# A decoder layer on one core: the summed weights of the first pair of queries are loaded ahead of the turned x1

## The chip, the core and the metric

The kernel runs on one core of a Trainium2 chip. A core has a matrix engine (TensorE, PE in the profile; its weight loads are shown as PEld), a vector engine (VectorE, DVE), a scalar engine (ScalarE, ACT), a general engine (GpSimd, POOL) and a queue engine (SyncE, SP) that here only issues transfers. Transfers are carried out by 16 DMA engines that all queues share. The metric is the time of one execution on the device in microseconds (us); the figure of a kernel is the median of its runs.

## The reference

One layer of a decoder, all in float32, with 8 sequences of 256 tokens and a width of 1024:

```python
x = _layernorm(x + attn(x, wq, wk, wv, wo))                     # causal, 32 heads of 32, 8 key heads, rotary
x = _layernorm(x + xattn(x, ctx, ctx, pos, mask, Wq, Wk, Wv, Wo))  # 32 heads of 128, 8 key heads, rotary, masked
x = _layernorm(x + ffn(x, ...))                                 # 256 memory slots: top 8, softmax, a gate
```

In the cross-attention the queries are `x @ Wq` with `Wq` of 1024 x 4096, and keys and values are `ctx @ Wk` and `ctx @ Wv` of 1024 x 1024. Then `out = softmax(q k / sqrt(128), masked) v` and `out @ Wo`, with `Wo` of 4096 x 1024.

## The kernel before

The work is staged in one pass over the self-attention (64 steps: 8 sequences of 8 steps) and one over the cross-attention (128 heads: 4 quarters of 512 tokens, 32 heads each). The first stage also computes, beside its own work, the keys and values of the cross-attention. The result of the first stage after its normalisation is called x1. It is turned tile by tile (`turn`: L397 transposes on TensorE, L398 copies on VectorE and ScalarE, L404 stores on ScalarE's queue) into x1T, since a projection wants the contracted dimension on the partitions.

Projections of the cross-attention save one multiplication in eight: two 128-wide outputs and two halves of the tokens are computed with seven block products instead of eight (`seven`, a scheme of Strassen's kind). The products are called p1, p2, p6, p5, p3, p7, p4, in this order. The token side needs the blocks B11, T3, B22, B21 of x1T (`load_blocks`, four loads of 512 KB, L642) and the sums T1, T2, T3, T4 of them (L646 to L649, on GpSimd for the first quarter). The weight side needs three kinds of tiles: the plain weights `a` of the pair's first output (p1 and p2), two tiles of summed weights `s24` and `s31` (p6 and p3; p5 and p7), which GpSimd has computed and stored in DRAM during the first stage, and half a tile of plain weights of the second output (p4). Each product is 4 matmuls of 128 x 128 by 128 x 256, which the profile counts as 8 (L757), into one bank of PSUM. What frees the bank is a copy on ScalarE for p1 (L776) and additions on VectorE for the others (L763). Two finished halves make a query of 512 tokens, which VectorE rotates with cos and sin (L730 to L734).

A pair of queries whose `seven` is called with `eager=True` loads `a` when its list of products is made, and not in p1. This is so for the first pair alone: `xa_early` makes it at the end of step 61, right before the loads of x1T, of cos and sin and of the first keys. The products themselves come later: p1, p2, p6, p5 at the end of step 62 and p3, p7, p4 with the first three of the next pair at the start of step 63.

The order of the work on TensorE, GpSimd and SyncE in the first stage is that of the program text (`manual_schedule`); VectorE's and ScalarE's is set by a scheduler, and GpSimd's last loads of the residual x1 (L119) belong to the second stage and are placed by it too. SyncE works through its queue strictly in order: a load that waits for a free buffer holds all loads behind it. Weights, turned tiles and a few others share one ring of 9 buffers of 512 KB (`w4`). The framework gives transfers issued by SyncE and ScalarE eight completion counters in turn, and a transfer waits until the previous holder of its counter has landed.

Around the change SyncE's queue has, in this order: plain weights of the first pair, x1T (4 loads), cos, sin, keys kT, `sa_wo` (4 loads of 512 KB for the last output projection of the self-attention, L364), the two summed tiles of the first pair, half a plain tile for p4, the plain weights of the second pair, its first summed weights, the mask (read by the mask bias, L695), its second summed weights. x1T is loaded into memory that the first stage's early pool gives back, so that its first load waits for the last work of that pool.

## Time and profile before

| | |
|---|---|
| runs | 3465.23, 3473.19, 3473.85 us; median 3473.19 |
| profiled execution | 3463.37 us, span 3461.6 us |
| TensorE busy | 3369.3 us, 97% of the span |
| VectorE, ScalarE, GpSimd busy | 61%, 35%, 30% |
| granted TensorE clock, mean | 0.988 |
| bytes moved | 626 MB, 181 GB/s over the span |

The profile is of one execution. An engine's busy time is a sum over the whole span, so it says which engine bounds the kernel and not what a single place costs. For that there are the chain of waits (the work that ended last, followed back from the end, each piece to what released it), the timeline of an engine or a queue, the waits summed by who waited for whom, and the busy times, granted clock and transfer rate of chosen stretches. The change touches the place where the first stage gives way to the second, 1100 to 1260 us after the start.

### The profile page before, as it was taken

The page shows a single profiled execution, that of the slowest core. Times are in us where ns is not written, and L with a number is a line of the kernel's source. Part 1 is how long each engine was busy: PE and PEld are TensorE (multiplying, and loading weights), DVE is VectorE, ACT ScalarE, POOL GpSimd, SP SyncE. Part 2 cuts the span into 40 slices and gives each one's busy share as a digit, 9 for nine tenths or more (in the row PEclk, how much of TensorE's full clock was granted, in tenths as well). Part 3 has the DMA queues.
Part 4 walks back from the last instruction along what each step waited for, and adds up shares of the span by engine and source line. Part 5 has one row for each costly group of instructions (what it writes and reads, how often), then busy time and mean ns, then how long its engine had stood idle before and what let it go on. Part 6 is the DMA issues. An engine that isn't in the chain of part 4 may idle for free.

```text
span 3461.6 us, 71080 instructions
## 1 busy us (share of the span) xinstructions
PE 3369.3 (97%) x27811; PEld 2443.5 (71%) x27811; DVE 2109.8 (61%) x6003; ACT 1202.3 (35%) x4030; POOL 1044.9 (30%) x1363
## 2 busy tenths in 40 slices
PE   8999999999999799999999999999999999999996
PEld 6787778787777567777767667667667766766763
DVE  4655556565565455665685666675666666566556
ACT  3444334333443343333233332233333323333224
POOL 3444655666665121111221111112111212121112
PEclk9999999999999899999999999999999999999998
DMA  7777788787886464444544344444444544344442
GB/s 254 236 258 250 269 268 279 257 273 258 296 271 221 156 215 141 143 135 134 171 149 140 123 134 142 150 137 156 138 128 133 167 142 147 128 132 135 129 146 98
DMA packets 269710, 626.36 MB, mean 181 GB/s; under 512 B 28992, under 2 KB 99792, under 8 KB 268480
## 3 DMA queue, kind: packets, MB, share of 16 engines
q1 hardware_dynamic: 194832, 441.00, 38.9%
q0 software_dynamic: 50032, 154.66, 13.8%
q10 hardware_dynamic: 24512, 26.15, 2.2%
q8 instruction: 221, 3.62, 0.4%
q14 instruction: 113, 0.93, 0.1%
HBM read 526.93 MB, written 94.77 MB: 180 GB/s over the span
## 4 chain that ended last, share of the span: by engine, by line
PE 87%; DVE 6%; DMA 2%; ACT 2%; POOL 2%; issue 2%; SPq 0%; POOLq 0%; DVEq 0%; ACTq 0%
PE mm L757 26%; PE mm L963 20%; PE mm L214 7%; PE mm L910 7%; PE mm L373 6%; PE sc L859 6%; PE mm L751 5%; PE sc L339 3%; PE mm L1241 2%; PE mm L243 1%; PE sc L273 1%; PE mm L1018 1%; POOL acc L992 1%; ACT att L295 1%; DMA w<-in_sa_wq 0%
## 5 line engine op out<-in xcount | busy, mean ns | idle before, releaser
L757 PE MATMUL mm<-x1T,w 128*128 128x256 f32 x3584 | 851.9, 382 | 13.7 <-DMA w<-xa_wq_sums 10.8
L757 PEld LDWEIGHTS mm<-x1T,w 128*128 128x128 f32 x3584 | 676.9, 190 | 199.0 <-issue 94.8
L963 PE MATMUL mm<-w,xoS 128*128 128x512 f32 x992 | 449.2, 595 | 0.0
L873 ACT ACTIVATE xatt<-xatt,nmax 128x256 f32<-128x256 f32 x512 | 257.2, 503 | 508.1 <-DVE nmax L868 496.2
L676 POOL DMA_DIRECT2D v<-v x256 | 150.9, 596 | 735.1 <-PE mm L910 617.1
L963 PE MATMUL mm<-w,xoT 128*128 128x512 f32 x744 | 338.1, 596 | 5.3 <-ACT xoT L918 4.1
L963 PEld LDWEIGHTS mm<-w,xoS 128*128 128x128 f32 x992 | 184.9, 190 | 193.1 <-issue 170.9
L214 PE MATMUL mm<-xT,w 128*128 128x256 f32 x1280 | 305.0, 395 | 3.1 <-DMA xT<-in_xT 2.9
L763 DVE TENSOR_TENSOR half<-mm,half 128x256 f32<-128x256 f32 x288 | 119.7, 416 | 291.1 <-PE mm L757 273.2
L214 PEld LDWEIGHTS mm<-xT,w 128*128 128x128 f32 x1280 | 245.4, 196 | 54.8 <-issue 19.0
L910 PEld LDWEIGHTS mm<-xat,v 32*128 32x128 f32 x8192 | 244.3, 187 | 53.4 <-issue 29.3
L929 POOL TENSOR_TENSOR xoS<-xoT 128x512 f32<-128x512 f32 x62 | 79.0, 1274 | 671.8 <-ACT xoT L918 671.5
L910 PE MATMUL mm<-xat,v 32*128 32x128 f32 x8192 | 270.2, 278 | 5.4 <-DVE acc L970 4.4
L295 ACT ACTIVATE att<-att,nmax 128x128 f32<-128x128 f32 (+1 forms) x512 | 225.5, 442 | 143.0 <-DVE nmax L290 142.8
L859 PE MATMUL sc<-kT,qT 128*128 128x256 f32 x1024 | 262.7, 380 | 0.0
L879 ACT ACTIVATE xatt<-xatt,rec 128x256 f32<-128x256 f32 x512 | 231.1, 499 | 88.0 <-DVE rec L877 87.6
L918 ACT COPY xoT<-mm 128x128 f32<-128x128 f32 x512 | 98.0, 276 | 470.2 <-PE mm L910 439.2
L763 DVE TENSOR_TENSOR raw<-mm,half 128x256 f32<-128x256 f32 x384 | 159.1, 414 | 159.3 <-PE mm L757 118.3
L423 POOL TENSOR_TENSOR ws<-ws 128x256 f32<-128x256 f32 x320 | 242.1, 757 | 26.2 <-DMA ws<-in_xa_wk 5.7
L963 PEld LDWEIGHTS mm<-w,xoT 128*128 128x128 f32 x744 | 138.7, 190 | 148.1 <-issue 127.3
L893 DVE STREAM_TRANSPOSE xat<-xatt 128x512 f32<-128x512 f32 x256 | 180.8, 707 | 74.6 <-ACT xatt L879 71.9
L373 PE MATMUL mm<-sa_wo,sa_oT 128*128 128x512 f32 x512 | 224.8, 592 | 0.0
(230 smaller groups left out, 4859.9 us busy)
## 6 DMA issues: line engine op xcount, KB each, us to landing
w<-xa_wq_sums SPq DMA_DIRECT2D x128, 512.0 KB, 3.6
w<-xa_wo_sums SPq DMA_DIRECT2D x124, 512.0 KB, 3.6
w<-in_xa_wo SPq DMA_DIRECT2D x97, 512.0 KB, 4.2
w<-in_sa_wq SPq DMA_DIRECT2D x64, 512.0 KB, 9.1
sa_wo<-in_sa_wo SPq DMA_DIRECT2D x64, 512.0 KB, 7.0
w<-in_xa_wq SPq DMA_DIRECT2D x64, 512.0 KB, 3.5
v<-v POOLq DMA_DIRECT2D x256, 128.0 KB, 3.1
w<-xa_wk_sums SPq DMA_DIRECT2D x32, 512.0 KB, 8.5
```

What stands on the lines that cost most here:

```text
L214: nc.tensor.matmul(ps[:, :S], lhsT=lhs[:, k, :], rhs=xT[:, k, :], start=(k == 0), stop=(k == KC - 1),)
L295: nc.scalar.activation(att[:, jj, lo:hi], att[:, jj, lo:hi], AF.Exp, bias=nmax[:, i : i + 1], scale=-1.0, accum_out=sums[:, i : i + 1],)
L373: nc.tensor.matmul(ps, lhsT=oTs[b * KC + c][:, tt * P : (tt + 1) * P], rhs=wos[b, half][c // 2][:, c % 2, :], start=(c == 0), stop=(c == K ...
L423: nc.gpsimd.tensor_tensor(out, in0, in1, op)
L757: nc.tensor.matmul(ps[:, :S], lhsT=w[:, k, :], rhs=rhs[:, k, :], start=(k == 0), stop=(k == 3))
L763: nc.vector.tensor_tensor(out, in0, in1, ALU.add)
L859: nc.tensor.matmul(sc[:, qt, :], lhsT=qT[:, q0 : q0 + P], rhs=kT[:, b * S : (b + 1) * S], start=True, stop=True,)
L873: nc.scalar.activation(att[:, qt, :], att[:, qt, :], AF.Exp, bias=nmax[:, qt : qt + 1], scale=-1.0, accum_out=sums[:, qt : qt + 1],)
L879: nc.scalar.activation(att[:, qt, :], att[:, qt, :], AF.Identity, bias=0.0, scale=rec[:, qt : qt + 1])
L893: self.nc.vector.transpose(self.ats[M, b][:, :, u].rearrange("p c t j -> p t c j"), self.atts[H][b].rearrange("p t (c j) -> p t c j", j=32),)
L910: nc.tensor.matmul(banks[i][:, :P], lhsT=v[rows, c, :], rhs=at[rows, c, :], start=(c == 0), stop=(c == BLOCKS - 1),)
L963: nc.tensor.matmul(ps, lhsT=oT[lhs][:, u, off + p * P : off + (p + 1) * P], rhs=w[:, u, :], start=(u == 0), stop=(u == 1),)
```

## The change

For the pair made with `eager=True` the two tiles of summed weights are now loaded where the plain ones are, when the list of products is made; p6 and p5 load them only for the other pairs. The loads themselves, their sizes and the products stay as they are. On SyncE's queue the two loads move from behind `sa_wo` to directly behind the plain weights, ahead of x1T.

```diff
         now = {}
         if eager:
             now["a"] = self.weights([P, KC, XA_D], self.a[name][2 * m])
+            for i, sums in enumerate(("s24", "s31")):
+                now[sums] = self.weights([P, KC, XA_D], self.wsums[name, m][i])
...
         def p6():
-            now["s24"] = self.weights([P, KC, XA_D], self.wsums[name, m][0])
+            if not eager:
+                now["s24"] = self.weights([P, KC, XA_D], self.wsums[name, m][0])
             ps = product(now["s24"][:, :4, :], "T2")
...
         def p5():
-            now["s31"] = self.weights([P, KC, XA_D], self.wsums[name, m][1])
+            if not eager:
+                now["s31"] = self.weights([P, KC, XA_D], self.wsums[name, m][1])
             ps = product(now["s31"][:, 4:, :], "T1")
```

In the changed program three more things stand elsewhere, as the scheduler and the turn of the counters set them: on GpSimd the load of x1's third residual tile (L119) comes ahead of the block sum T2 and not behind T4; on VectorE the mask bias comes behind the rotation of the second query and not ahead of that of the first; and the counters of the transfers from x1T to `sa_wo` are those of two places further on.

## The prediction

> **What bounds the kernel now.** I read the page first, then the chain of waits in order of time around the first pair of queries, then SyncE's queue, then stretches of the clock. The page says that TensorE is the bound, so a stall of TensorE is worth about its length:

> ```profile
> span 3461.6 us, 71080 instructions
> PE 3369.3 (97%) x27811; PEld 2443.5 (71%) x27811; DVE 2109.8 (61%) x6003; ACT 1202.3 (35%) x4030; POOL 1044.9 (30%) x1363
> PE 87%; DVE 6%; DMA 2%; ACT 2%; POOL 2%; issue 2%; SPq 0%; POOLq 0%; DVEq 0%; ACTq 0%
> ```

> The chain in order of time, from 1150 to 1203 us (columns: start, length, what). Two transfers follow one another with no TensorE work between them: a turned tile of x1 is stored, then summed weights are loaded, and only then does L757 go on.

> ```profile
> 1157.43 11.93 DMA x1T<-w
> ...
> 1171.34 9.08 DMA w<-xa_wq_sums
> 1180.42 0.14 issue
> 1180.56 14.00 PE mm L757 x56
> ```

> SyncE's queue in order of time (start, length of issuing, line, transfer): it is silent from 1104.85 to 1156.04; it stops again from 1160.15 to 1169.38; the summed weights are issued behind four loads of `sa_wo`.

> ```profile
> 1104.52 0.33 SPq L109 DMA_DIRECT2D w<-in_xa_wq  x1
> 1156.04 2.03 SPq L642 DMA_DIRECT2D x1T<-x1T  x4
> 1158.11 0.91 SPq L664 DMA_DIRECT2D cos<-tables  x1
> 1159.06 0.45 SPq L664 DMA_DIRECT2D sin<-tables  x1
> 1159.55 0.60 SPq L668 DMA_DIRECT2D kT<-kT  x1
> 1169.38 1.92 SPq L364 DMA_DIRECT2D sa_wo<-in_sa_wo  x4
> 1171.34 1.20 SPq L109 DMA_DIRECT2D w<-xa_wq_sums  x2
> 1172.58 1.21 SPq L109 DMA_DIRECT2D w<-in_xa_wq  x2
> ```

> SyncE's own waits name the second stop (total, times, longest): the store of the turned tile.

> ```profile
> SPq L364 <- DMA x1T<-w: 9.2, 1, 9.2
> ```

> The stretches (TensorE busy, granted clock, DMA share, GB/s): the idle time from 1169.8 to 1180.56 halves the clock, and it stays halved until 1184; the transfers meanwhile run full at 408 GB/s.

> ```profile
> 1142.00:1146.00 4.00, 1.03 (x7) 1.00 0.93 327
> 1146.00:1153.00 7.00, 5.36 (x100) 0.53 0.10 40
> 1173.00:1180.50 7.50, 0.00 (x0) 0.55 1.05 408
> 1180.50:1184.00 3.50, 3.44 (x8) 0.51 1.05 399
> 1184.00:1194.50 10.50, 10.50 (x52) 1.00 0.43 161
> ```

> Work that stands ready meanwhile, out of the timeline: it sets how early the next products could run.

> ```profile
> 1170.41 2.35 POOL L649 TENSOR_TENSOR x1T<-x1T 128x1024 f32<-128x1024 f32 x1
> 1171.15 0.56 ACT L398 COPY w<-mm 128x512 f32<-128x512 f32 x1
> 1173.01 0.35 ACT L776 COPY half<-mm 128x256 f32<-128x256 f32 x1
> ```

> **The change, part by part.** No instruction is added. Two 512 KB loads move.

> *The two loads.* They go directly behind the plain weights, ahead of x1T, cos, sin, kT and `sa_wo`. Their buffers were last read by a value product of step 58 and by the query projection L214, whose matmuls run from 1118.05 to 1121.77, so both are issued by about 1122, inside SyncE's silence. The eight such loads issued here before took 7.8 us (median) to land; by 1132 they are there. DMA share was 0.54 in 1118 to 1122 and 0.00 in 1122 to 1130, and TensorE waited for no transfer from 1100 to 1156. I take 0. If that cover were gone, 1.05 MB at 0.4 MB/us costs 2.6 us; a gain below 0 is excluded, since nothing there waits for them.

> *Queue places.* Transfers of SyncE and ScalarE take eight completion counters in turn, and each waits for the last holder of its counter. That is the 9.2 us wait: the first `sa_wo` shared one with the store issued at 1157.43. Two places further on, it is the sin load that stands behind that store, so sin, kT and all behind them go out when it lands: at 1169.36, or up to 1 us earlier, as 0.5 MB no longer competes with it. Sin is first read after p3, at about 1175.8, and lands by about 1172.5 (3 us of cover); kT is read at 1215.

> *POOL.* In the changed order the load of x1's third residual tile (0.55 us of issuing) stands ahead of the block sum T2. It waits for transposes that end at 1165.56, so T2 starts at 1166.2 instead of 1165.76 and ends at 1168.55, before p6 wants it at 1169.8: 0, with 1.2 us of cover. Its 512 KB now moves with the `sa_wo` loads from their start.

> *VectorE.* The mask bias (0.69 us) moves behind the second rope; VectorE is not on the path, and the bias is first read at 1216.83: 0.

> *TensorE, where the gain is.* A product takes 1.73 us at full clock. Before, seven (p6, p5, p3, p7, p4 and the next pair's p1, p2) ran from 1180.56 to 1194.48: 13.92 us against 7 x 1.73 = 12.1, so the halved clock cost 1.8. After:
> - p6 starts at 1169.8. p5 needs a bank freed by ScalarE at 1171.71, so 1171.8. p3 needs the L776 copy (1173.36), so 1173.5. p7 follows at 1175.3 and ends at 1177.0. Nothing here waits longer than 0.3 us.
> - p4 is late next: its plain weights (256 KB) were not moved. Ahead of them on the queue, after the restart, stand sin, kT and four `sa_wo`: 0.26 + 0.26 + 2.10 MB, and 0.26 of their own, 2.88 MB. Before, the first summed weights ended after 2.10 + 0.52 = 2.62 MB and landed at 1180.42. So p4's weights land 0.26 MB (0.65 us) later against a restart 0 to 1 us earlier: 1180.1 to 1181.1. Bounds from both sides: 1178.5, if the residual load is out of the way early, and 1183.5, if it and the second store keep half the engines. I take 1180.2, since the byte count is nearest to the row measured.
> - p4 and two more products are 5.2 us, plus the clock. TensorE idles 3.2 us (1177.0 to 1180.2). The row of 1142 to 1153 shows what such a gap does: idle from 1142.87 to 1145.85, and then 0.53. So again 1.8: end at 1187.2 instead of 1194.48.

> [...]

> Later work hangs on TensorE itself: `sa_wo` is reloaded when L373 has read it (1210.34), the values when the last transposes are done (1231.52), so it moves along. Sum: -7.3 us (-0.21%).

> **Against which time.** The profiled execution took 3463.37 us, 1.8 more than its span. The runs shown are 3465.23, 3473.19 and 3473.85, median 3473.19: with the profiled one, two levels some 9 us apart. -7.3 gives 3456.1 at the profiled level and 3465.9 from the median. A median of three new runs can fall at either, so I start from the mean of the four, 3468.9: 3462.

> **The rivals.** 0.3% (10.4 us) is about what a measurement of this kernel can tell from no change.
> - *Clock kept.* A gap of 3.2 us stays at full clock: -7.3 - 1.8 = -9.1, 3454 to 3464. [...] Against: the row above. [...]
> - *The whole stall goes.* p4's weights land by 1177.0: end 1182.2, -12.3, about 3457 to 3461. Against: 2.88 MB after 1169 at 0.4 MB/us needs 7.2 us and some 2 us to start and land.
> - *Given back.* The residual load and the second store take half the engines, p4 starts at 1183.5: -4, about 3465 to 3469. For it: before, this load began late, after `sa_wo`. Against: it is only 0.5 MB.
> - *Slower.* The second summed load waits for its buffer and holds x1T and all behind it in SyncE's queue, which is in order. Each us that the buffer comes free after 1156.04 then costs 1 us, less the 7.3: slower from 1163.3 on. If the buffer were the first turned tile's (read until 1169.36) it is 13.3 - 7.3 = +6; if the second one's (issued at 1171.74, 14.6 us to land), +23, some 3492. Against: the changed order gives it a buffer read last at 1121.77. This is also how the change could fail to do what it says.

> **How the numbers follow.** Likeliest 0.52, clock kept 0.17, whole stall 0.12, given back 0.11, slower 0.08. Faster by over 0.3% means under 3462.8: half of the likeliest (its lower level) 0.26, of clock kept 0.10, whole stall 0.12, given back 0.02: 0.50. Within: 0.26 + 0.07 + 0.09, and 0.02 of the slower case: 0.44. Slower by over 0.3%: 0.06. The range goes from the lower level of clock kept, with some of whole stall (3453), to the upper level of given back with spread (3473).

> **What the changed profile would show.** Right: on SyncE, the plain and two summed loads between 1104 and 1122, and a wait of the sin load for the store x1T<-w; TensorE's 10.8 us wait for `xa_wq_sums` gone, and one of about 3 us for `in_xa_wq` at L759 (757 before) in its place, at 1177 to 1180; p2 of the next pair done near 1187. Wrong: the wait for `in_xa_wq` missing or over 6 us, a wait of TensorE for x1T of over 1 us, or x1T issued after 1157. The time would be wrong where the two levels of the runs fall otherwise than evenly.

## The result, and the profile after

| | before | changed |
|---|---|---|
| median of 20 runs each | 3466.93 us (3461.80 to 3476.04) | 3462.39 us (3456.96 to 3467.74) |
| ratio, 95% interval | | 0.9986 (0.9979 to 0.9992) |
| profiled execution, span | 3463.37, 3461.6 us | 3462.11, 3460.3 us |

The change makes the kernel faster by 4.5 us, or 0.14%. That is real, as the interval shows, but smaller than the 0.3% that I had named as what can be told from no change. The forecast was 3462.0.

Line numbers of the stage are 2 to 4 higher in the changed kernel (L757 is L759, L776 is L778). First its page: TensorE is still the bound, at the same share.

```profile
span 3460.3 us, 71082 instructions
PE 3370.6 (97%) x27811; PEld 2443.5 (71%) x27811; DVE 2110.6 (61%) x6003; ACT 1202.4 (35%) x4030; POOL 1046.9 (30%) x1363
```

SyncE's queue in order of time (start, length of issuing, line, transfer), to be read against the rows of before in the prediction:

```profile
1104.83 0.33 SPq L109 DMA_DIRECT2D w<-in_xa_wq  x1
1115.27 7.18 SPq L109 DMA_DIRECT2D w<-xa_wq_sums  x2
1157.41 2.02 SPq L642 DMA_DIRECT2D x1T<-x1T  x4
1159.48 1.01 SPq L664 DMA_DIRECT2D cos<-tables  x1
1170.22 0.33 SPq L664 DMA_DIRECT2D sin<-tables  x1
1170.59 0.47 SPq L668 DMA_DIRECT2D kT<-kT  x1
1171.11 1.97 SPq L364 DMA_DIRECT2D sa_wo<-in_sa_wo  x4
1173.12 2.41 SPq L109 DMA_DIRECT2D w<-in_xa_wq  x2
```

The summed weights are issued in the silence and out by 1122.5. The queue's long stop is still there, 1160.5 to 1170.2, but the sin load is now the one that stands in it, with all of `sa_wo` and p4's plain weights behind it. SyncE's own waits name the same store for it (9.7 us, against 9.2 us in before).

TensorE's timeline at the same place (start, length, line, operation; in brackets the idle time ahead and what ended it), of before and then of the changed kernel. The first row of each starts with p1, the last is the next pair's p6:

```profile
1165.35 4.45 PE L757 MATMUL mm<-x1T,w 128*128 128x256 f32 x16
1180.56 14.00 PE L757 MATMUL mm<-x1T,w 128*128 128x256 f32 x56 [10.75 <-DMA w<-xa_wq_sums]
1195.90 1.99 PE L757 MATMUL mm<-x1T,w 128*128 128x256 f32 x8
```

```profile
1166.72 11.87 PE L759 MATMUL mm<-x1T,w 128*128 128x256 f32 x48
1183.52 6.83 PE L759 MATMUL mm<-x1T,w 128*128 128x256 f32 x24 [4.94 <-DMA w<-in_xa_wq]
1191.70 1.99 PE L759 MATMUL mm<-x1T,w 128*128 128x256 f32 x8
```

Six products (p1, p2, p6, p5, p3, p7) now run without a stop. Then TensorE waits 4.94 us for p4's weights, where before it waited 10.75 us for the summed ones. The chain of waits (start, length, what) tells the same: a store, then a load, then L759 again, only with other weights.

```profile
1158.80 11.40 DMA x1T<-w
...
1173.12 10.26 DMA w<-in_xa_wq
...
1183.52 6.83 PE mm L759 x24
```

TensorE entered the stage 1.4 us later in this execution. Most of that is the granted clock: the 16 matmuls of L214 just ahead took 5.76 us here, at a mean granted clock of 0.64, and 4.71 in before, at 0.78. So I compare lengths from the start of p1. To the start of the next pair's p6 it took 30.5 us before (1165.35 to 1195.90) and 25.0 here (1166.72 to 1191.70): 5.6 us less.

### The profile page after: what moved, and what is told of

Same layout as the page of the kernel before. It is cut to its first block, busy times and chain, and to the rows that moved or that the text cites. A ratio compares the mean times of both kernels' runs of the same rounds, so it can differ in the third digit from the quotient of the medians.

```text
span 3460.3 us, 71082 instructions
## 1 busy us (share of the span) xinstructions
PE 3370.6 (97%) x27811; PEld 2443.5 (71%) x27811; DVE 2110.6 (61%) x6003; ACT 1202.4 (35%) x4030; POOL 1046.9 (30%) x1363
## 4 chain that ended last, share of the span: by engine, by line
PE 61%; DVE 5%; POOL 1%; ACT 1%; issue 1%; DMA 1%; SPq 0%; POOLq 0%; ACTq 0%; DVEq 0%
PE mm L759 21%; PE mm L967 20%; PE mm L914 7%; PE sc L863 6%; PE mm L1245 2%; PE mm L373 2%; PE mm L1022 1%; PE mm L214 1%; PE mm L753 1%; POOL acc L996 1%; DVE res L996 0%; DVE t L732 0%; PE mm L1262 0%; DVE ln_st L126 0%; DVE xat L897 0%
## 5 line engine op out<-in xcount | busy, mean ns | idle before, releaser
L759 PE MATMUL mm<-x1T,w 128*128 128x256 f32 x3584 | 853.6, 382 | 9.3 <-DMA w<-in_xa_wq 4.9
L759 PEld LDWEIGHTS mm<-x1T,w 128*128 128x128 f32 x3584 | 678.1, 191 | 195.1 <-issue 89.4
L214 PE MATMUL mm<-xT,w 128*128 128x256 f32 x1280 | 305.6, 395 | 2.8 <-DMA xT<-in_xT 2.2
L214 PEld LDWEIGHTS mm<-xT,w 128*128 128x128 f32 x1280 | 246.1, 196 | 54.4 <-issue 18.4
L883 ACT ACTIVATE xatt<-xatt,rec 128x256 f32<-128x256 f32 x512 | 231.2, 499 | 88.1 <-DVE rec L881 87.7
L373 PE MATMUL mm<-sa_wo,sa_oT 128*128 128x512 f32 x512 | 224.8, 592 | 0.0
```

What stands on the lines that cost most here:

```text
L214: nc.tensor.matmul(ps[:, :S], lhsT=lhs[:, k, :], rhs=xT[:, k, :], start=(k == 0), stop=(k == KC - 1),)
L373: nc.tensor.matmul(ps, lhsT=oTs[b * KC + c][:, tt * P : (tt + 1) * P], rhs=wos[b, half][c // 2][:, c % 2, :], start=(c == 0), stop=(c == K ...
L759: nc.tensor.matmul(ps[:, :S], lhsT=w[:, k, :], rhs=rhs[:, k, :], start=(k == 0), stop=(k == 3))
L883: nc.scalar.activation(att[:, qt, :], att[:, qt, :], AF.Identity, bias=0.0, scale=rec[:, qt : qt + 1])
```

## The experiments

Each group of runs has its own runs of before: the median of before was 3472.72 us for the first four, 3470.19 for the next four and 3466.89 for the last four. Ratios are against those.

**The changed kernel again (e1).** No edit.

> The changed kernel once more, unaltered, for a second profile of the place. Theory A (queue place): TensorE waits for the plain weights of p4 (in_xa_wq) in every execution, for 3 to 5 us, and the time is 4 to 5 us under the kernel before. The four sa_wo loads ran at 0.30 MB/us in the first profile of the changed kernel and at 0.39 before; if that belongs to the change, they do it again and the wait is again about 4.9 us; if it was chance, the rate is back near 0.39 and the wait is about 3.2 us.

Measured: 3469.19 us, ratio 0.9991 (0.9982 to 0.9999). Same direction, less sure. Its profile shows how much p4's wait differs between executions:

```profile
1172.15 12.01 PE L759 MATMUL mm<-x1T,w 128*128 128x256 f32 x48
1186.75 5.42 PE L759 MATMUL mm<-x1T,w 128*128 128x256 f32 x24 [2.59 <-DMA w<-in_xa_wq]
```

The wait is 2.59 us here against 4.94, and the 24 matmuls behind it take 5.42 us, at a granted clock of 1.00, against 6.83 at a mean of 0.79. From p1 to the next p6: 21.4 us.

**Only half of the change (e2).** `s24` is loaded early, `s31` in p5 as before.

```diff
-            for i, sums in enumerate(("s24", "s31")):
+            for i, sums in enumerate(("s24",)):
                 now[sums] = self.weights([P, KC, XA_D], self.wsums[name, m][i])
```

> Of the two summed tiles only s24 is loaded ahead; s31 stays behind sa_wo. Theory A (the product whose weights stand behind sa_wo is the one that stalls): p6 runs at once, then TensorE waits 8 to 10 us for s31 ahead of p5, and the gain is under 1.5 us against the kernel before: one tile alone buys almost nothing. Theory B (every tile moved buys its own share of the bytes, 0.5 MB at 0.4 MB/us): about half of the gain of both, some 2.3 us.

Measured: 3472.70 us, ratio 0.9993 (0.9985 to 1.0002), which is too wide to tell the two theories apart; the trace does. TensorE's timeline:

```profile
1192.92 12.16 PE L759 MATMUL mm<-x1T,w 128*128 128x256 f32 x48 [9.48 <-DMA w<-xa_wq_sums]
```

p6 runs, and then p5 waits 9.48 us. The stall does not shrink with the number of loads that are moved: it moves to the first weights that are still behind the stop. From p1 to the next p6 it is 29.2 us, 1.3 less than before. The queue shows one thing more: the load that stands in the stop is the first of `sa_wo` in before, kT here (for 9.1 us) and sin in the changed kernel. Each load that goes ahead of x1T shifts it by one place, as completion counters taken in turn would have it. The traces of before and of the changed kernel name the counter of each transfer: SyncE and ScalarE use 100 to 107, the store has 101 in both, and so has the load that stands in the stop, the first of `sa_wo` in before and sin in the changed kernel.

**`sa_wo` later (e3, e4).** e3 is the changed kernel, e4 the kernel before, each with the four last loads of `sa_wo` issued behind the plain weights of p4 and of the next pair. In the diff the first line stands at the end of step 62, behind its products.

```diff
+                load_out(b, 0)
...
-            elif c == 6:
+            elif c == 6 and b + 1 < B:
```

> The changed kernel, and the four sa_wo loads of the last output projection are issued behind the plain weights of p4 and of the next pair. Theory A (p4 waits because its weights stand behind 2.1 MB of sa_wo): no wait of TensorE over 1 us between p1 and the next pair's p2, so the stretch ends 5 to 6.5 us earlier than in the changed kernel; 9 to 11 us under the kernel before. Theory C (the transfers are the limit whatever their order): the wait moves to the next pair's summed weights or to sa_wo, and the time is within 2 us of the changed kernel.

> The kernel before, without the change, but with the four sa_wo loads behind the first pair's summed weights, the plain weights of p4 and those of the next pair. Theory A (being behind sa_wo costs the most of the wait): the summed weights go out when the turned tile's store lands, and p6 starts 3 to 4 us after that, so TensorE's 10.8 us wait shrinks to 3 to 5 us, some 6 to 8 us under the kernel before: more than the change itself brings. Theory D (being behind the store's counter costs the most): the wait stays at 8 us or more, 0 to 3 us gained.

Measured: e3 3465.13 us, ratio 0.9973 (0.9963 to 0.9982); e4 3467.26 us, ratio 0.9980 (0.9972 to 0.9989). TensorE's timeline, of e3 and then of e4:

```profile
1173.38 17.05 PE L760 MATMUL mm<-x1T,w 128*128 128x256 f32 x72
1194.86 1.97 PE L760 MATMUL mm<-x1T,w 128*128 128x256 f32 x8 [3.01 <-DMA w<-xa_wq_sums]
```

```profile
1184.92 14.01 PE L758 MATMUL mm<-x1T,w 128*128 128x256 f32 x56 [3.38 <-DMA w<-xa_wq_sums]
```

In e3 all of the pair and the next pair's p1 and p2 run through, and the wait comes at the next pair's p6. In e4 the old wait falls from 10.8 to 3.38 us though the summed weights stand where they stood. Both loads stand in the same queue behind the same stop; e4, without the change, comes out no slower than the change alone, which has 0.9991 beside it (e1).

**The stop itself (e5).** The changed kernel, with one store issued by GpSimd, so that it takes no completion counter of SyncE's and ScalarE's turn (what GpSimd issues has 108 to 115 in the traces of before and of the changed kernel).

```diff
-            nc.scalar.dma_start(out=self.x1T_d[q][:, :, i * P : (i + 1) * P], in_=turned)
+            queue = nc.gpsimd if (b, tt) == (B - 2, 0) else nc.scalar
+            queue.dma_start(out=self.x1T_d[q][:, :, i * P : (i + 1) * P], in_=turned)
```

> Changed kernel, but the store of the turned x1 ahead of the stage (line 404, the first of the last two) is issued by GpSimd, so that no load of SP's queue takes its completion counter in turn. Theory A (SP's stop of 10 us behind that store's counter sets when p4's weights land): sin goes out right behind cos, kT and the first load of sa_wo too, the later loads of sa_wo stand behind pieces of x1T at most (until about 8 to 10 us after cos, as estimated from where these land now); p4's plain weights are issued 4 to 6 us earlier against p1 than in the changed kernel, its wait of 2.6 to 4.9 us falls below 1 us, and the ratio to before is 0.9965 to 0.998 (7 to 12 us). Theory B (the volume of the transfers sets it, not the queue): the loads of kT and sa_wo now run beside x1T's, p1 starts 2 to 4 us later, and the ratio is that of the changed kernel, 0.9985 to 0.9995.

Measured: 3455.20 us, ratio 0.9963 (0.9950 to 0.9977). SyncE's queue and TensorE:

```profile
1159.73 0.53 SPq L665 DMA_DIRECT2D cos<-tables  x1
1160.30 0.57 SPq L665 DMA_DIRECT2D sin<-tables  x1
1160.92 1.22 SPq L669 DMA_DIRECT2D kT<-kT  x1
1162.18 6.50 SPq L364 DMA_DIRECT2D sa_wo<-in_sa_wo  x4
1170.48 1.11 SPq L109 DMA_DIRECT2D w<-in_xa_wq  x2
```

```profile
1166.70 12.03 PE L760 MATMUL mm<-x1T,w 128*128 128x256 f32 x48
1179.59 5.42 PE L760 MATMUL mm<-x1T,w 128*128 128x256 f32 x24 [0.86 <-DVE t L734]
```

The stop is gone: from the start of cos to that of sin it is 0.57 us, not 10.74. The store itself still takes 9.4 us to land (11.4 in the changed kernel), and sin is out 8.4 us before it has; what is gone is the wait for it. `sa_wo` still waits a while for pieces of x1T, whose counters it now shares in the turn of eight (its four loads take 6.50 us to issue, 1.97 in the changed kernel), and p4's weights are issued 3.8 us after the start of p1 (6.4 in the changed kernel), so the move is 2.6 us and not the 4 to 6 that I had expected. It suffices: p4 waits for no transfer, and x1T is not late for it. From p1 to the next p6: 19.7 us. Theory A holds, with a ratio slightly below the 0.9965 to 0.998 that it gave; theory B falls.

**Both (e6, and once more as e10), and both without the change (e9).** The edits of e5 and of e3; e9 has them on the kernel before.

> Changed kernel with both: the store issued by GpSimd as in e5, and the loads of sa_wo issued behind p4's and the next pair's plain weights as in e3. Theory A: no wait for p4's weights, and the next pair's summed weights, which cost 3.0 us of waiting in e3, land up to 8 us earlier, so that the stretch from p1 to the next pair's p6 has no wait over 1 us; 0 to 3 us better than e3, ratio to before 0.9965 to 0.9975. Theory B (volume): as e3 or worse by the 1 to 3 us that x1T's pieces come later, ratio 0.9973 to 0.998.

> The kernel before, without the change, with the two edits of e6 (store issued by GpSimd, loads of sa_wo last). Theory A (SP's stop behind the store's counter is the whole cause, and loading the summed weights ahead is one of several ways around it): the first pair's summed weights are issued at the landing of x1T's first pieces instead of 12 us later, p6 and p5 wait 0 to 3 us in all in place of 10.75, and the ratio to before is 0.9955 to 0.9975, within 0.1% of e6. Theory B (these loads must be ahead of the stage in any case): p6 waits 4 us or more, and the ratio is 0.9975 or above.

> The kernel of e6 once more, beside e9 on the same chip. Theory A: ratio 0.995 to 0.997, at most 0.1% below e9. Theory B: 0.1% or more below e9.

Measured: e6 3452.41 us, ratio 0.9955 (0.9941 to 0.9968). On another chip e10 3454.57 us, 0.9965 (0.9953 to 0.9977), beside e9 3457.94 us, 0.9970 (0.9960 to 0.9981). TensorE's timeline of e6, then of e9:

```profile
1163.51 17.41 PE L761 MATMUL mm<-x1T,w 128*128 128x256 f32 x72
1182.26 1.99 PE L761 MATMUL mm<-x1T,w 128*128 128x256 f32 x8
```

```profile
1170.80 1.99 PE L759 MATMUL mm<-x1T,w 128*128 128x256 f32 x8 [0.62 <-DMA x1T<-x1T]
1174.85 14.01 PE L759 MATMUL mm<-x1T,w 128*128 128x256 f32 x56 [2.05 <-DMA w<-xa_wq_sums]
1190.20 1.99 PE L759 MATMUL mm<-x1T,w 128*128 128x256 f32 x8
```

e6 has no wait left between p1 and the next p6 (18.8 us) and beats both kernels; its ratio is better than either theory had it, that of e10 lies within theory A's range. e9 has 2.7 us of waits and half a clock behind them (22.8 us). Theory A's bounds for e9 held (waits of 0 to 3 us, a ratio of 0.9955 to 0.9975). Once the stop is gone the change itself is still worth 3.9 us of that stretch (18.9 in e10); the medians differ by 3.4 us, but the intervals of the ratios overlap.

**Is it TensorE that slows the loads? (e7)** In the changed kernel the loads of `sa_wo` ran at 299 GB/s, where the loads of before ran at 396 to 408 while TensorE stood still. e7 leaves out three of the four steps of the inner sum in the first pair's p6, p5, p3 and p7.

```diff
-                for k in range(4):
+                ks = 1 if eager and block in ("T2", "T1", "B22", "T3") else 4
+                for k in range(ks):
                     nc.tensor.matmul(
-                        ps[:, :S], lhsT=w[:, k, :], rhs=rhs[:, k, :], start=(k == 0), stop=(k == 3)
+                        ps[:, :S], lhsT=w[:, k, :], rhs=rhs[:, k, :], start=(k == 0), stop=(k == ks - 1)
                     )
```

> Changed kernel, with one of four steps of the inner sum left out of none but computed alone in the first pair's p6, p5, p3 and p7: three of four matmuls of each of these products are left out, so the queries of the first pair are not those of the reference; loads, additions and orders stay. TensorE then works about 6 us less between p2 and p4. Theory A (the loads of sa_wo run at 0.30 MB a us in the changed kernel against 0.39 to 0.40 before because TensorE works beside them): they run at 0.38 to 0.40, p4's weights land 10.5 to 11.5 us after SP's restart. Theory B (something else, as the neighbouring transfers or GpSimd's additions, slows them): 0.30 and 13 us, as in the changed kernel.

Measured: one run, 3460.83 us; the trace is what counts. Stretches while `sa_wo` is loaded (start and end, length, busy time of TensorE, of its weight loads, of VectorE, ScalarE, GpSimd, then granted clock, DMA share, GB/s), of the changed kernel, of e7 and of e6:

```profile
1171.20:1177.90 6.70, 6.70 (x32) 5.76 (x32) 4.16 (x13) 3.54 (x13) 3.60 (x2) 1.00 0.97 299
```

```profile
1172.00:1178.00 6.00, 3.21 (x12) 1.55 (x10) 3.96 (x14) 3.62 (x13) 3.69 (x2) 1.00 0.86 258
```

```profile
1164.50:1168.90 4.40, 4.40 (x17) 3.38 (x16) 3.77 (x14) 4.40 (x18) 4.38 (x4) 0.74 1.07 387
```

With TensorE busy for half the time e7 is no quicker: 258 GB/s, and p4's weights land 13.1 us after the restart. In e6 the loads run at 387 GB/s although TensorE, ScalarE and GpSimd work all the time. The theory that a busy TensorE slows them falls, and e6 speaks against the other engines too; theory B only says that it is something else, and what it is stays open.

**The kernel before once more (e8), the changed one twice more (e11, e12).** In the first two profiles of the changed kernel something came back later: p1 of the pair of queries at about 1258 us waited 2.58 and 2.17 us, and half a clock followed (in the first 0.50 from 1258.07 to 1261.48), where before had 1.20 us and a clock of 1.00. Together that gave back 2.7 to 2.8 us.

> The kernel before once more, for its trace: the wait ahead of p1 of the pair of queries at about 1258 us, 1.20 us there and 2.2 and 2.6 us with half a clock behind it in the two profiles of the changed kernel. Theory A (chance: the transfers of that load differ from one execution to the next): any value from 0.8 to 2.6 us. Theory B (the change moved something onto that load): 1.2 us within 0.2, and no half clock. The wait of 10.75 us for the summed weights ahead of the next product should come again within 0.5 us, with half a clock behind it.

> The changed kernel once more, for its trace: the wait ahead of p1 of the pair at about 1258 us, 2.58 and 2.17 us with half a clock behind it in its two profiles, 1.0 to 1.4 us without one in seven profiles of other kernels. Theory A (chance of that load's transfers): 1.0 to 1.5 us and no half clock. Theory B (the changed kernel's own): 2 us or more again. The wait for p4's weights: 2.5 to 5 us; half a clock behind it only if a whole window of 3.41 us of the clock's grid lies in it.

> As the run before it, a fourth trace of the changed kernel, with the same two theories and numbers.

Measured: one run each, 3464.07, 3461.56 and 3461.52 us. TensorE's timeline at that place, of the first profile of the changed kernel and of its third:

```profile
1258.61 3.38 PE L759 MATMUL mm<-x1T,w 128*128 128x256 f32 x8 [2.58 <-ACT xatt L883]
```

```profile
1258.00 1.97 PE L759 MATMUL mm<-x1T,w 128*128 128x256 f32 x8 [1.03 <-DMA w<-in_xa_wq]
```

The third and fourth profile of the changed kernel wait 1.03 and 0.99 us and keep the clock (p1 took 1.97 us in both, 3.38 in the first); e8 waits 1.12. e10, another kernel, waits 1.70 and loses the clock (p1 took 3.59 us). The first row names ScalarE's L883 as what ended the wait, but in the third profile p1 runs at 1258.00, before L883 starts there (1258.52), so p1 does not need it. What p1 needs is the load of its weights: it landed 4.48 us after its issue in the first profile (at 1258.47) and 2.94 us in the third (at 1257.86). The same kernel shows both, so this is the spread of one load's transfers from one execution to the next. Four profiles are too few to say that the change does not make a long wait likelier. p4's wait came as 4.85 and 5.04 us in the two new profiles, here of the fourth:

```profile
1184.11 8.19 PE L759 MATMUL mm<-x1T,w 128*128 128x256 f32 x24 [5.04 <-DMA w<-in_xa_wq]
```

The wait of before came again as 10.30 us. The four profiles of the changed kernel take 25.0, 21.4, 26.5 and 26.4 us from p1 to the next p6, mean 24.8; the two of before 30.5 and 30.8. That is 5.8 us less.

## Why the prediction was right, and where it was not

- *The two loads cost nothing:* right. They were issued from 1115.27 to 1122.45, x1T at 1157.41, and no wait for them is left in the stage. The slower rival (a buffer late, x1T held) did not come: SyncE was silent until x1T.
- *Queue places:* right. Sin took over the place behind the store and waited 9.7 us. e5 shows the cause by taking it away. The restart, 3.0 to 3.6 us after the start of p1 in the four profiles, lies where I put it (1169.36, or up to 1 us earlier, against p1 at 1165.35).
- *GpSimd and VectorE at 0:* right. T2 ran from 1167.80, was there for p6, and all six products ran without a stop; the mask bias made nothing wait.
- *p4 is late next:* right in place, wrong in size. The row of before has 11.0 us from the restart to the landing of the first summed weights; with 0.65 us for 0.26 MB more the sum is 11.7 us, and the 1180.2 that I took is its early end. p4's weights took 13.2, 11.5, 13.0 and 13.4 us. Over these stretches all queues together moved 3.8 to 4.3 MB, mean 4.0, which is what before's row (3.7 MB) and the added 0.26 MB make, so the byte count was right. The rate was not: 325, 332, 308 and 298 GB/s against 336 in the row. The loss lies mainly in the first 7.5 us, with 225 to 298 GB/s against 300; there the loads of `sa_wo` ran at 299 GB/s and less (239 in the fourth profile). So p4 waited 4.9, 2.6, 4.9 and 5.0 us instead of 3.2, inside the bounds that I gave (a landing up to 1183.5, a wait of 6.5 us), up to about halfway to the late one, and not for the reason named there: the residual load had its last packet 0.7 to 1.2 us after the restart, and the second store's packets moved only from over 7 us after it on. This is the term that was mis-sized, by some 1.2 us on the mean of the four waits, 4.35 us.
- *The clock:* the size, 1.8 us, was that of before's 10.8 us stall; that a gap of 3.2 us would cost as much was read from a row where a 2.97 us gap (ahead of L339 at 1145.85) had halved the clock (0.53 in 1146 to 1153). Measured it was two half-clock periods in two profiles (the 24 matmuls took 8.47 and 8.19 us instead of 5.42), one in another (6.83), none in e1 (5.42): 3.0, 2.8, 1.4 and 0, on the mean 1.8. The mean is the number that I took, by luck; as a rule of gap length the step fails. In the three profiles that lost the clock one whole period of the clock's grid (3.413 us, below) was idle (0.00 us busy); in e1 none was (2.18 and 2.05 us busy in the two that share the gap), and the clock stayed at 1.00. What the traces show of it is below.
- *Clock kept* (-9.1) thus came true in one of four profiles, e1, with 9.2 us less than before. *The whole stall goes* did not, in any. *Given back* (-4, p4 at 1183.5) is close to what three of the four profiles show, 4.0, 4.1 and 5.6 us less than the 30.5 of before.
- *Sum:* -7.3 predicted for the stretch, -5.8 there on the mean of the profiles, -4.5 measured over the whole kernel. The 2.7 to 2.8 us that two of the four profiles lost at 1258 would be 1.4 on the mean and make up the difference; the interval of the ratio (2.8 to 7.3 us) is too wide to say more. That later work moves along held in two profiles of four.
- *Against which time:* I read four runs as two levels, half and half, and started from their mean, 3468.9. The 20 runs of before run from 3461.8 to 3469.5 without a gap, and only five lie above 3472; in the next group they lie evenly between 3467.6 and 3480.5. The base was 2.0 us too high and the gain 2.8 us too large, and the two nearly cancelled. That 3462.0 came within 0.4 us of the median is owed to that, and is luck. A chance of 0.50 for faster by over 0.3% was too much: the gain I had worked out was 0.21%, and the rest was to come from the levels.

## What to carry to other kernels

Where a strictly ordered queue stops, moving the loads that wait behind it only passes the wait to the next load in line: e2 moved one tile and kept nearly all of the stall, the change moved two and kept some 40% of it (4.35 of 10.75 us). Ask what the queue stops for. Here one edit, which sent a slow store over a queue with counters of its own, gained more together with the change (0.9963) than the change alone (0.9986). Ordering the loads by first use on top took another 0.9 us out of the stretch (e6), which the ratios do not resolve. The store's edit alone, on the kernel before, was not run.

## What the runs showed of the hardware

| busy time in a period | clock in it | next one half | next one full |
|---|---|---|---|
| under 1.2 us | full | 50 | 0 |
| 1.2 to 2.0 us | full | 70 | 40 |
| 2.0 to 2.8 us | full | 16 | 285 |
| over 2.8 us | full | 0 | 13142 |
| under 2.8 us | half | 58 | 0 |
| 2.8 to 3.4 us | half | 45 | 27 |
| over 3.4 us | half | 4 | 111 |

So a gap costs by where it falls. In the mixed rows something else decides too, and what it is was not found: a period busy for 1.49 us kept the clock in e3, one busy for 1.71 us lost it in e10. Two adjoining periods in e3, whose gap of 3.01 us is shared between them, and then three in the fourth profile of the changed kernel, where one period is idle throughout (start and end, length, busy time of TensorE, its weight loads, VectorE, ScalarE, GpSimd; clock, DMA share, GB/s):

```profile
1189.53:1192.94 3.41, 2.31 (x101) 1.57 (x99) 0.62 (x1) 0.00 (x0) 0.00 (x0) 1.00 1.06 393
1192.94:1196.35 3.41, 1.49 (x7) 1.37 (x8) 0.08 (x1) 0.00 (x0) 0.00 (x0) 1.00 0.55 213
1196.36:1199.77 3.41, 2.89 (x120) 2.25 (x119) 1.87 (x4) 0.85 (x4) 0.00 (x0) 1.00 0.03 10
```

```profile
1179.49:1182.90 3.41, 0.00 (x0) 0.00 (x0) 1.79 (x4) 0.00 (x0) 0.00 (x0) 1.00 1.08 402
1182.90:1186.31 3.41, 2.20 (x5) 1.85 (x6) 0.00 (x0) 0.00 (x0) 0.00 (x0) 0.50 1.06 393
1186.31:1189.72 3.41, 3.41 (x9) 2.70 (x8) 1.77 (x3) 0.00 (x0) 0.00 (x0) 0.50 0.75 289
```

e3 keeps the clock, at 1.00. In the other the idle period halves the next one; that one is busy for only 2.20 us, so the clock stays halved for one more. The gap that I had gone by falls almost whole into one period: in 1143.00 to 1146.41 of before TensorE was busy for 0.40 us, and the next period had a clock of 0.50. The gap of 2.58 us at 1258 did the same with 1.38 us of busy time in 1254.66 to 1258.07. A period that is idle throughout, as I had it in the expectation of e11, is not needed for that: of the periods at full clock all 50 that were busy for under 1.2 us, and 86 more up to 2.8 us, were followed by half a clock.

**The same loads run at 239 to 299 GB/s in one place and at 387 to 408 in another.** In the slow stretches most packets of 2 KB take 84 ns as elsewhere (84 to 87), but 7 to 9 in a hundred take 150 ns or more, some over 1 us; in the fast stretches it is under 1 in a hundred. It lasted for some 7 us after the restart in the changed kernel and under 3 us in before. A busy TensorE does not explain it (e7: 258 GB/s with TensorE busy for 3.21 of 6.00 us), the other engines hardly can (e6: 387 GB/s with ScalarE and GpSimd busy for 4.40 and 4.38 of 4.40 us), and a cause was not found.
